# Another order for the parts of a software-pipelined stage: layer 1's cross-attention and experts

## The chip, the cores and the metric

The kernel runs on one core of one Trainium2 chip. The core has five engines with an instruction queue each: TensorE (PE, with the weight loads PEld beside it), VectorE (DVE), ScalarE (ACT), GpSimd (POOL) and SyncE (SP), which here only starts DMAs. An engine takes its instructions in the order of its queue; engines wait for each other by semaphores. The metric is the device time of one execution in microseconds.

## What is computed

A decoder of two layers on x of 16 x 256 tokens of 128 numbers, with a context of 16 x 64 tokens. Each layer adds to x an attention, a cross-attention with the context, and a mixture of experts, each on a layer norm of x. The change lies in the last two of layer 1:

```python
def _L1_xattn_ref(x, latents, w_q, w_kv, w_out, b_out):   # x: the context; latents: layernorm(x)
    q = latents @ w_q.T
    k, v = jnp.split(x @ w_kv.T, 2, axis=-1)              # 16 heads of 8, 64 keys
    ...
    attn = jax.nn.softmax(jnp.einsum('blhd,bshd->bhls', q, k) * SCALE, axis=-1)
    out = jnp.einsum('bhls,bshd->blhd', attn, v).reshape(B, L, DIM)
    return out @ w_out.T + b_out

def _L1_ffn_ref(x, gate_w, wg, wu, wd, sg, su, sd):       # 8 experts, the best two of each token
    top_w, top_i = jax.lax.top_k(jax.nn.softmax(xt @ gate_w, axis=-1), TOP_K)
    ...                                                   # cw: the two shares, else 0
    h = jax.nn.silu(einsum('th,ehi->eti', xt, wg)) * einsum('th,ehi->eti', xt, wu)
    moe = einsum('eth,te->th', einsum('eti,eih->eth', h, wd), cw)
    return moe + (jax.nn.silu(xt @ sg) * (xt @ su)) @ sd
```

## The kernel before, in words

All of x stays in SBUF, as eight chunks of 512 tokens (two sequences, four tiles of 128 tokens). Layer 0, layer 1's attention and layer 1's last stage follow each other; the last stage works on the eight chunks. In it every token is put through all experts, two experts to a product, and the routing's shares are multiplied in.

The stage is cut into *parts*, small functions of one engine each, which are called in the order of a list written out by hand, PLAN (L2076). An entry such as `E3:0` is a part and its distance in chunks: in iteration c the part E3 is called for chunk c, `h2:2` for chunk c-2, `S0:-1` for chunk c+1. The loop goes over iterations and, in each, over the list; entries whose chunk does not exist are left out. The calls' order is the order in each engine's queue (the block is scheduled by hand, and only where it meets the attention before it are instructions mixed). So the list sets, for each engine on its own, what stands behind what; between engines the framework puts the semaphores.

The parts that the text speaks of, by engine, with their lines:

- PE: S0 to S3 scores of a tile (L1816), T transposes of the probabilities, in two halves of a tile (L1876: T30 is tile 3, half 0), V products with the values (L1894), Y output projection (L1910), P transposes of the shares (L1863), xt and xq transposes and queries of a chunk (L1465, L1477), ft transposes and fl router products (L1932, L1941), fw transposes of the routing weights (L1976), h0 to h4 the gate and up products (L2004: h0 the shared expert, h1 to h4 two experts each), d0 to d3 the down products of a tile (L2022).
- DVE: G the greatest score (L1823), B the subtraction of it (L1827), R sums (L1849, L1850), O and X what comes out of V and Y (L1902, X adds to x: L1916), xs and fs layer norm statistics (L1447, L1448), fg the choice of two experts (L1948, then L160 to L178: reduces, and products and comparisons of 128 x 32 numbers, each on the result of the one before), fq the shares (L1959 to L1969), m gate times up (L2011), z the sum that is written out (L2031).
- ACT: E the exponential (L1835), C copies of T out of PSUM (L1885), U of P (L1870), xc, xQ, fc, fW copies (L1469, L1483, L1936, L1981; fW also starts, on SP, the two DMAs that spread the routing weights over partitions, L1983, L1988), fn normalisation (L1923), a0 to a4 Silu of the gate (L2008), fe the exponential of the routing (L1953). Exponential and Silu come from two tables, and a load (ACT_TABLE_LOAD) stands between them.
- POOL: A first additions of a tile's probabilities (L1841, L1842), Q the shares of the heads (L1855), K keys spread by heads (L1489), xr and fr roots for the layer norms (L1453 to L1460), xb adds the output's bias to x (L1472), k1 to k4 the multiplication of the experts' products by the routing weights (L2017).

PSUM: the scores hold four banks, one tile `sx` for two tiles' scores; h holds a bank for the gate and one for up (free again after a and m); everything else that PE writes (xt, xq, T, V, Y, P, ft, fl, fw, d) takes turns in two buffers, `misc`. Each of these parts therefore waits until what the part two places before it wrote has been copied out: by ACT for T, P, xt, xq, ft and fw, by DVE for V, Y, fl and d.

Of the kernel before, what the change touches and what calls it, by code (L numbers as in the profile page):

```python
# [62 lines left out]
def kernel(ctx: ExitStack, tc: tile.TileContext, a: dict, out: bass.AP):  # L63
# [1734 lines left out]
    with ExitStack() as ph:  # L1798
# [271 lines left out]
        for n in range(NPE + 1):  # L2070
# [3 lines left out]
            PARTS[f"k{n}"] = lambda c, n=n: weighted(c, n)  # L2074

        PLAN = (  # L2076
            "A0:0 a1:2 fs0:1 V1:1 z1:3 O1:1 xq:-1 xs0:-1 S3:0 K0:-2 R0:0 Y1:1 m1:2 xQ:-1 X1:1 "
            "T21:0 fs1:1 C21:0 A1:0 h2:2 T10:0 G3:0 Q0:0 a2:2 xb:-1 m2:2 T11:0 fr:1 C10:0 h3:2 "
            "T00:0 C11:0 T01:0 B3:0 k2:2 a3:2 C00:0 S0:-1 R1:0 m3:2 k1:2 xr:-1 xs1:-2 C01:0 "
            "T20:0 fn:1 G0:-1 C20:0 Q1:0 A2:0 h4:2 a4:2 k3:2 B0:-1 m4:2 P0:0 V0:0 U0:0 O0:0 "  # L2080
            "k4:2 ft:1 S1:-1 Y0:0 fc:1 fl:1 R2:0 h0:1 G1:-1 a0:1 X0:0 Q2:0 d3:2 fg:1 z3:2 E3:0 "
            "T30:0 fe:1 B1:-1 A3:0 C30:0 d0:2 E0:-1 xt:-2 m0:1 z0:2 S2:-1 fq:1 xc:-2 R3:0 Q3:0 "
            "T31:0 d2:2 C31:0 fw:1 G2:-1 z2:2 h1:1 E1:-1 P1:0 K1:-2 fW:1 U1:0 d1:2 B2:-1 E2:-1 "
        )
        room["m"] = ps_m
        plan = [part.split(":") for part in PLAN.split()]
# [66 lines left out]
```

## Time and profile before

| what | value |
|---|---|
| median of 9 runs | 1445.43 us (1443.76 to 1450.71) |
| the profiled execution's own time | 1447.09 us |
| its span in the profile | 1445.4 us |
| granted TensorE clock over the span | 0.98 |
| layer 1's last stage in the trace | from about 1190 us to the end |
| busy in 1275 to 1300 us | PE 23.82, DVE 20.44, ACT 16.65, POOL 17.28 of 25 us |

How it is read. The profile is one execution; times are in us from its start. Lines such as "L1876 PE MATMUL tx<-ident,px" are the line of the code, the engine, the operation, and what it writes and reads. An arrow in brackets behind a number of a timeline is the idle time of the engine before the instruction, and what ended it. The chain of waits follows the work that ended last back from the end of the program, at each step to what released it.

### The profile page before, as it was taken

What the parts mean: (1) busy time and instruction counts of PE and PEld (TensorE: products, weight loads), DVE (VectorE), ACT (ScalarE), POOL (GpSimd) and SP (SyncE); (2) the same over time, 40 slices, a digit from 0 to 9 for tenths busy, and PEclk for the clock granted to TensorE, in tenths of its full rate; (3) what the DMA queues carried; (4) which work ended last, traced back from release to release, by engine and by line L of the source; (5) the groups of instructions that cost most, each with busy time, mean ns of one, the idle gap of its engine ahead of it and who ended that gap; (6) DMA issues with size and microseconds to landing.
All of it is one profiled execution on the core that took longest, in us unless ns stands there. A gap on an engine that the chain in (4) does not pass through costs nothing.

```text
span 1445.4 us, 37905 instructions
## 1 busy us (share of the span) xinstructions
PE 1360.0 (94%) x13169; PEld 993.3 (69%) x13169; DVE 1114.1 (77%) x4508; ACT 950.7 (66%) x2569; POOL 727.6 (50%) x1160
## 2 busy tenths in 40 slices
PE   6999999999999999899999969999999987899997
PEld 4777776767676766589999956666666654566664
DVE  6676777777677767777878758999999968888863
ACT  5777675757576767344333319999999975666652
POOL 7454657474747564545433334443334216677643
PEclk9999999999999999899999988999999998999999
DMA  6772000000000000357677520000000000121122
GB/s 157 237 250 61 2 13 5 7 10 4 14 2 16 2 16 2 101 181 221 211 245 238 179 63 16 17 12 15 17 2 2 2 2 1 30 68 44 38 67 52
DMA packets 79757, 94.82 MB, mean 66 GB/s; under 512 B 19488, under 2 KB 62752, under 8 KB 79568
## 3 DMA queue, kind: packets, MB, share of 16 engines
q1 hardware_dynamic: 64736, 45.20, 11.8%
q10 hardware_dynamic: 10512, 38.28, 8.4%
q0 software_dynamic: 4320, 8.92, 1.8%
q8 instruction: 106, 1.74, 0.5%
q14 instruction: 83, 0.68, 0.2%
HBM read 63.72 MB, written 28.65 MB: 64 GB/s over the span
## 4 chain that ended last, share of the span: by engine, by line
PE 65%; ACT 17%; DVE 10%; DMA 2%; issue 2%; POOL 2%; SPq 0%; POOLq 0%; DVEq 0%; ACTq 0%
ACT p L1670 8%; PE pqk L406 8%; PE s L461 5%; PE o L533 5%; PE y L438 4%; PE g L1316 4%; PE u L1316 4%; PE y L1334 4%; PE pv L423 3%; PE t L1688 3%; PE t L513 2%; PE s L1648 2%; PE o L1712 2%; ACT pT L1699 2%; PE g L2004 2%
## 5 line engine op out<-in xcount | busy, mean ns | idle before, releaser
L486 ACT ACTIVATE p<-p,nm 128x128 f32<-128x128 f32 (+1 forms) x512 | 227.8, 447 | 138.6 <-DVE nm L474 136.4
L497 POOL TENSOR_SCALAR p<-p,rs 128x128 f32<-128x128 f32 (+1 forms) x512 | 210.5, 427 | 163.9 <-DVE rs L495 139.3
L1670 ACT ACTIVATE p<-p,nm 128x256 f32<-128x256 f32 x512 | 220.9, 507 | 9.6 <-DVE nm L1659 8.5
L1659 DVE CUSTOM_DVE_ANT_0 p<-s,strip 128x256 f32<-128x256 f32 x512 | 186.7, 419 | 19.6 <-PE s L1648 18.4
L474 DVE CUSTOM_DVE_ANT_0 p<-s,strip 128x128 f32<-128x128 f32 (+1 forms) x512 | 158.2, 347 | 2.2 <-PE s L461 2.2
L522 DVE COPY pT<-t 128x384 f32<-128x384 f32 x256 | 130.7, 552 | 27.8 <-PE t L513 26.9
L1344 POOL DMA_INDIRECT rows_out<-yr,to x71 | 68.5, 964 | 118.1 <-DVE yr L1343 111.0
L461 PE MATMUL s<-k,q 64*128 64x128 f32 (+1 forms) x1024 | 118.5, 350 | 0.0
L1688 PEld LDWEIGHTS t<-ident,p 64*128 64x128 f32 x2048 | 80.0, 140 | 54.2 <-issue 15.7
L533 PE MATMUL o<-pT,v 128*64 128x256 f32 (+1 forms) x1024 | 112.2, 340 | 0.5 <-ACT oT L543 0.5
L461 PEld LDWEIGHTS s<-k,q 64*128 64x128 f32 x1024 | 67.1, 186 | 62.5 <-issue 56.3
L1688 PE MATMUL t<-ident,p 64*128 64x64 f32 x2048 | 102.2, 232 | 7.8 <-ACT pT L1699 2.8
L432 DVE COPY v<-pv 128x512 f32<-128x512 f32 x64 | 44.1, 689 | 73.7 <-PE pv L423 73.6
L486 ACT ACTIVATION_READ_ACCUMULATOR p<-p,nm 128x1 f32 x512 | 96.8, 189 | 0.0
L1324 ACT ACTIVATE gs<-gs 128x512 f32<-128x512 f32 x71 | 44.7, 629 | 77.7 <-DVE gs L1323 64.2
L1648 PE MATMUL s<-k,q 32*128 32x256 f32 x1024 | 88.3, 418 | 4.5 <-POOL k L1568 4.5
L1530 POOL TENSOR_SCALAR ve_a<-mv_a 128x2 f32<-128x2 f32 x16 | 3.7, 229 | 164.3 <-DVE mv_a L1525 164.3
L1699 ACT COPY pT<-t 128x512 f32<-128x512 f32 x144 | 81.2, 588 | 5.5 <-PE t L1688 4.7
L513 PEld LDWEIGHTS t<-ident,p 64*128 64x128 f32 x1536 | 70.5, 139 | 19.1 <-DVE v L432 3.6
L533 PEld LDWEIGHTS o<-pT,v 128*64 128x64 f32 x1024 | 62.4, 136 | 28.2 <-ACT oT L543 0.9
L809 POOL DMA_INDIRECT rows_in<-xn,slot_in x64 | 63.7, 995 | 33.0 <-DVE nm L474 19.2
L1699 DVE COPY pT<-t 128x512 f32<-128x512 f32 x112 | 75.3, 684 | 5.9 <-PE t L1688 5.9
(341 smaller groups left out, 3403.5 us busy)
## 6 DMA issues: line engine op xcount, KB each, us to landing
gu<-in_L_ffn_gate_up_w ACTq DMA_DIRECT2D x71, 512.0 KB
rows_in<-zero SPq DMA_DIRECT2D x131, 130.0 KB
spread<-wrows SPq DMA_DIRECT2D x16, 512.0 KB
xr<-rows_in SPq DMA_DIRECT2D x71, 65.0 KB
y<-rows_out SPq DMA_DIRECT2D x16, 256.0 KB
x<-in_x SPq DMA_DIRECT2D x8, 256.0 KB
out_x<-yo SPq DMA_DIRECT2D x16, 128.0 KB
rows_out<-yr,to POOLq DMA_INDIRECT x71, 3.3
```

The costliest lines, as they stand in the source:

```text
L406: nc.tensor.matmul(ps[:, u, :], w[:, (pair + u) * P : (pair + u + 1) * P], xnT[b // 2][:, lo : lo + N], start=True, stop=True,)
L461: nc.tensor.matmul(ps_of[b, h][:, cols], q[rows, u2, iq], k[rows, u2, 0:nk], start=True, stop=True,)
L474: nc.vector.tensor_tensor_reduce(out=pr[:, cols], in0=ps[:, cols], in1=strip[:, h, P : 2 * P] if it == 0 else strip[:, h, :], scale=1.0, s ...
L486: nc.scalar.activation(pr[:, cols], pr[:, cols], AF.Exp, bias=nm[:, it : it + 1], scale=-1.0, accum_out=sm[:, it : it + 1],)
L497: nc.gpsimd.tensor_scalar(pr[:, cols], pr[:, cols], rs[:, it : it + 1], 1.0, ALU.mult, ALU.mult)
L522: nc.vector.tensor_copy(pT_of[u][:, :, :, r, :], tp_of[u][r])
L533: nc.tensor.matmul(po[rows, c0:N], v[:, jt, h % 8 * DH : (h % 8 + 1) * DH], pT[:, 0:N] if jt == 0 else pT[:, N:], start=(jt == 0), stop=(j ...
L1648: nc.tensor.matmul(ps_of[b, h][:, it, :], q[rows, it * P : (it + 1) * P], k[rows, s4, :], start=True, stop=True,)
L1659: nc.vector.tensor_tensor_reduce(out=pr[:, it, :], in0=ps[:, it, :], in1=strip1[:, h, (1 - it) * P : (1 - it) * P + N], scale=1.0, scalar= ...
L1670: nc.scalar.activation(pr[:, it, :], pr[:, it, :], AF.Exp, bias=nm[:, it : it + 1], scale=-1.0)
L1688: nc.tensor.transpose(halves[r][:, k, jt, it, :], pr[rows, it, jt * P : (jt + 1) * P], ident[rows, rows],)
L1699: copy(pT_of[u, i][:, :, :, :, r, :].rearrange("p k j i c -> p (k j i) c"), tp_of[u, i][r].rearrange("p k j i c -> p (k j i) c"),)
```

## The change

Only the list PLAN is another one (L2076). It has the same 105 parts. Four distances change: A0 from 0 to -1 (it stands at the end of the list and no longer at the head, the same chunk either way), xb from -1 to 0, K0 from -2 to -3, K1 from -2 to -1. All else is order:

```diff
         PLAN = (
-            "A0:0 a1:2 fs0:1 V1:1 z1:3 O1:1 xq:-1 xs0:-1 S3:0 K0:-2 R0:0 Y1:1 m1:2 xQ:-1 X1:1 "
-            "T21:0 fs1:1 C21:0 A1:0 h2:2 T10:0 G3:0 Q0:0 a2:2 xb:-1 m2:2 T11:0 fr:1 C10:0 h3:2 "
-            "T00:0 C11:0 T01:0 B3:0 k2:2 a3:2 C00:0 S0:-1 R1:0 m3:2 k1:2 xr:-1 xs1:-2 C01:0 "
-            "T20:0 fn:1 G0:-1 C20:0 Q1:0 A2:0 h4:2 a4:2 k3:2 B0:-1 m4:2 P0:0 V0:0 U0:0 O0:0 "
-            "k4:2 ft:1 S1:-1 Y0:0 fc:1 fl:1 R2:0 h0:1 G1:-1 a0:1 X0:0 Q2:0 d3:2 fg:1 z3:2 E3:0 "
-            "T30:0 fe:1 B1:-1 A3:0 C30:0 d0:2 E0:-1 xt:-2 m0:1 z0:2 S2:-1 fq:1 xc:-2 R3:0 Q3:0 "
-            "T31:0 d2:2 C31:0 fw:1 G2:-1 z2:2 h1:1 E1:-1 P1:0 K1:-2 fW:1 U1:0 d1:2 B2:-1 E2:-1 "
+            "a1:2 xq:-1 V1:1 fs0:1 R0:0 z1:3 O1:1 S3:0 xs0:-1 m1:2 Y1:1 xQ:-1 X1:1 T21:0"
+            " C21:0 h2:2 T10:0 G3:0 fs1:1 a2:2 K1:-1 Q0:0 A1:0 fr:1 m2:2 T11:0 C10:0"
+            " h3:2 T00:0 B3:0 C11:0 a3:2 C00:0 xs1:-2 R1:0 m3:2 S0:-1 S1:-1 T01:0 T20:0"
+            " fn:1 G0:-1 C01:0 C20:0 A2:0 Q1:0 h4:2 R2:0 B0:-1 P0:0 V0:0 a4:2 U0:0 O0:0"
+            " m4:2 G1:-1 xr:-1 xb:0 k3:2 k2:2 k1:2 k4:2 ft:1 Y0:0 fc:1 fl:1 h0:1 E3:0"
+            " a0:1 X0:0 d3:2 fg:1 z3:2 d0:2 T30:0 fe:1 A3:0 K0:-3 Q2:0 C30:0 m0:1 z0:2"
+            " B1:-1 d2:2 xt:-2 fq:1 E0:-1 xc:-2 z2:2 R3:0 Q3:0 A0:-1 S2:-1 fw:1 T31:0"
+            " G2:-1 h1:1 E1:-1 fW:1 C31:0 P1:0 U1:0 d1:2 B2:-1 E2:-1"
         )
```

By engine, the middle of an iteration reads so in the built program:

- PE before: V1 xq S3 Y1 T21 h2 T10 T11 h3 T00 T01 S0 T20 h4 P0 V0 ft S1 Y0 fl h0 d3 T30 d0 xt S2 T31 d2 fw h1 P1 d1. After: xq V1 S3 Y1 T21 h2 T10 T11 h3 T00 S0 S1 T01 T20 h4 P0 V0 ft Y0 fl h0 d3 d0 T30 d2 xt S2 fw T31 h1 P1 d1.
- ACT before: ... U0 fc a0 E3 fe C30 E0 xc C31 E1 fW U1 E2. After: ... U0 fc E3 a0 fe C30 E0 xc E1 fW C31 U1 E2.
- POOL before: A0 K0 A1 Q0 xb fr k2 k1 xr Q1 A2 k3 k4 Q2 A3 Q3 K1. After: K1 Q0 A1 fr A2 Q1 xr xb k3 k2 k1 k4 A3 K0 Q2 Q3 A0.
- DVE before: fs0 z1 O1 xs0 R0 m1 X1 fs1 G3 m2 B3 R1 m3 xs1 G0 B0 m4 O0 R2 G1 X0 fg z3 B1 m0 z0 fq R3 G2 z2 B2. After: fs0 R0 z1 O1 xs0 m1 X1 G3 fs1 m2 B3 xs1 R1 m3 G0 R2 B0 O0 m4 G1 X0 fg z3 m0 z0 B1 fq z2 R3 G2 B2.

## The prediction

> **What bounds the kernel now.** I read the page first, for the share of each engine, and then the windows over stretches of the last stage (layer 1's cross-attention and experts, from about 1190 us to the end). The windows' columns are the length, then busy us and count of PE, PEld, DVE, ACT and POOL, the clock and the DMA.
>
> ```profile
> PE 1360.0 (94%) x13169; PEld 993.3 (69%) x13169; DVE 1114.1 (77%) x4508; ACT 950.7 (66%) x2569; POOL 727.6 (50%) x1160
> ```
> ```profile
> 1275.00:1300.00 25.00, 23.82 (x179) 15.74 (x178) 20.44 (x59) 16.65 (x28) 17.28 (x21) 1.00 0.15 39
> 1300.00:1325.00 25.00, 23.82 (x173) 15.85 (x172) 20.51 (x55) 16.71 (x28) 18.50 (x24) 1.00 0.13 31
> ```
>
> PE is busy 23.82 of 25 us at full clock: the stage is PE's. The chain of waits in order of time shows where the missing 1.18 us is.
>
> ```profile
> 1339.66 0.97 PE g L2004 x2
> ...
> 1341.27 1.28 ACT L1835
> ...
> 1342.57 1.16 ACT px L1835
> ...
> 1343.77 0.65 PE tx L1876 x4
> ...
> 1367.62 0.97 PE g L2004 x2
> ```
>
> An iteration is 1367.62 - 1339.66 = 27.96 us. ACT waits for the first expert product, does its Silu (a0), loads a table (the nameless 1.28 us), and only then comes the exponential E3, for which PE's transposes T30 wait. The waits from 1225 to 1350 us agree (us in total, times, longest).
>
> ```profile
> POOL half L1841 <- ACT px L1835: 19.9, 5, 4.9
> ...
> ACT gs L2008 <- PE g L2004: 12.9, 13, 2.5
> ...
> PE tx L1876 <- ACT px L1835: 7.0, 5, 2.3
> ```
>
> PE stalls 2.29 us in the stage's first full iteration (at 1232) and 1.18 us in six more. The first row matters as much: POOL waits for E3 too, up to 4.9 us. What DVE does meanwhile is the routing fg (L1948, L160 to L178), thirteen small dependent instructions, 2.73 us (1339.76 to 1342.49). The timelines of DVE and of POOL show why that idle POOL is worth something. First the end of the kernel, where POOL is not idle during fg; then the first iteration, where fq, the second half of the routing, meets POOL.
>
> ```profile
> 1415.28 1.32 DVE L162 TENSOR_TENSOR eq_f<-lgs_f,m_f 128x32 f32<-128x32 f32 x1
> 1416.63 0.19 DVE L163 TENSOR_TENSOR eq_f<-eq_f,rev 128x32 f32<-128x32 f32 x1
> ```
> ```profile
> 1411.61 4.95 POOL L2017 TENSOR_TENSOR hb<-hb,spread 128x512 f32<-128x512 f32 x4 [1.21 <-DVE hb L2011]
> ```
> ```profile
> 1232.61 0.98 DVE L1959 TENSOR_SCALAR w<-dm_f 128x4 f32<-128x4 f32 x1
> ...
> 1233.83 0.56 DVE L1961 TENSOR_TENSOR dm_f<-dm_f,w 128x4 f32<-128x4 f32 x1
> ```
> ```profile
> 1232.27 1.29 POOL L1841 TENSOR_TENSOR half<-px 128x512 f32<-128x512 f32 x1 [4.92 <-ACT px L1835]
> 1233.64 0.73 POOL L1842 TENSOR_TENSOR half<-half 128x256 f32<-128x256 f32 x1
> ```
>
> L162 takes 0.19 us elsewhere; here 1.32, and it ends at 1416.60, just behind POOL's last product (1416.56). L1959 (0.16 elsewhere) ends at 1233.59, behind POOL's 1233.56, and L1961 (0.16) at 1234.39, behind 1234.37. So a small DVE instruction of this kind (two SBUF inputs, or L1959's form) stands still until the POOL instruction under way ends. The reduces between them (L160, L167) and those that read PSUM run on at their usual lengths.
>
> **The change, part by part.** Same parts, so nothing is removed; the list moves them.
>
> *E3 before a0.* E3's input is long there, so it fills the 2.45 us in which ACT waited for the product: fc ends, table 1.28, E3 1.15, all before PE has done the first product pair and d3, d0 (0.81 + 1.80 + 1.12 + 1.12 = 4.85 us from the start of fl). The stall of 1.18 goes. The built program has 34 table loads for 22: two more in each of six iterations, 2 x 1.28 us of ACT. They lie before a0 and before fe, where ACT was waiting; ACT then stands about where it stood (C30 0.9 us after T30's start, xt's slot free 0.1 us before PE wants it). I cost them at nothing; without that cover they cost up to 2.56 us an iteration.
>
> *Small new waits on PE.* S1 leaves the place between ft and fl, and only Y0 (0.55) covers fc there. The last full iteration of before has no S1, and shows the price: from the start of V0 (1390.10) to fl (1392.43) 2.33 us for 1.00 + 0.58 + 0.55 of work, so +0.20. xq goes ahead of V1, so Y1 now waits for the PSUM slot of xq: U1, E2 1.15, table 1.29, a1 0.49, xQ 0.59 after P1 is 4.06 us, against d1 1.21, xq 1.05, V1 1.00 and S3 0.65: +0.15. Keys, S0 with S1, R0 and R2: their inputs are ready 0.3 us or more ahead, nothing. SP's copies keep their order; the weights land 9 us after fW (1238.28 to 1247.30), and the first product comes 15 after it (fW 5.8 ahead of X1, the product 9.6 behind X1, see below): 6 to spare, nothing.
>
> *POOL's order.* Count from X1 (L1916, at 1355.24 in before). In before fs1 ends 1.35 later and POOL's row of fr, products, xr, Q1, A2, products, Q2 ends at 1367.92, X1 + 12.68; fg's first L162 is issued at X1 + 12.92, and then POOL idles for E3. After: G3 stands ahead of fs1 (+1.10), so fs1 ends at 2.45. POOL: fr 2.06, A2 2.06, Q1 0.36, xr 1.32, xb 1.25 (moved here), and now all four products in a row, 4 x 1.25; the third ends at 13.34, the fourth at 14.59. As E3 is early, A3 follows at once (2.06), then K0 0.60 and Q2 0.37. PE from the end of Y1 to the end of fl is 12.45 + 0.20; X1 starts 0.6 behind Y1, so fl ends at X1 + 12.05. DVE must finish G1 and X0 first (V0's end, O0, m4, G1, X0 give 12.55); L162 is issued at about 12.95.
>
> So fg, until now beside an idle POOL, meets 4.7 us of POOL work in a row. Eight of its instructions can stand still. If each gets in behind the POOL instruction under way: L162 13.4, L163 14.7 (fourth product), L169 16.0 and L175 16.9 (A3), L162 17.5 (K0), L163 17.9 (Q2), the rest free: fg ends at 18.5 and not 15.3. z3 (0.29) follows, and frees the PSUM slot that T30 needs: T30 at 18.9, while PE is ready for it at 12.05 + 1.80 + 1.12 + 1.12 = 16.1. A stall of 2.8 where 1.18 went. d2 then waits for m0 and z0 behind z3 (19.8, PE at 19.4): +0.4.
>
> *Sum of an iteration:* -1.18 + 0.20 + 0.15 + 2.8 + 0.4 = +2.4 us. Six such (the last has no S, but the same row of POOL work): +14.2.
>
> *Ends.* First iteration: the stall of 2.29 goes, but fg meets A3, K0 and Q2, B1 stands behind fg, and S2 behind B1 comes at 1234.3 as before (1234.22): 0, between -2.3 and +1. The fill gains S1's place beside older work, -0.25. The last two iterations hold no A3 and no S, and hang on the copy of the weights to 1431.3 as before: 0. In all +14 on the profiled execution, whose own time is 1447.09 us (span 1445.4); that is 1.66 above the median, so 1445.4 + 14 = 1459.5.
>
> *Bounds of the disputed step.* That no row shows DVE waiting in a long row of POOL instructions leaves it open from both sides. Below: if fg is not held, it ends at 15.3, z3 at 15.6, T30 doesn't wait; -0.8 an iteration, -5 in all, about 1440. Above: if DVE gets in only when POOL runs dry (17.6), fg ends at 19.95, T30 at 20.3: stall 4.2, +3.8 an iteration, +23, 1468. I take the turn-by-turn value by its nearest row: L1959, issued within L1841, ended (1233.59) before L1842 began (1233.64).
>
> The Trainium skill (SBUF — State Buffer, "Who interferes with whom") says that a VectorE instruction with two SBUF inputs and a GpSimd instruction that reads SBUF exclude each other for the whole instruction, and that the order of issue decides who waits. The rows above show the first half; no run here shows the order of issue in a long row of GpSimd work. By that rule a waiting VectorE instruction is ahead of the next GpSimd one, which is the 1459.5; were the row of GpSimd work to keep the port, it would be the 1468.
>
> **The rivals.**
> - *E3's stall simply goes; fg finds POOL idle or isn't held.* 1440, faster. For it: the stall is real, and three of the stage's five meetings of DVE and POOL (1233.83, 1256.34, 1393.97) cost under 0.4 us. Against: A3 alone follows E3 by 0.05 us and covers 2.06 us of fg. It decides if POOL's row ends before X1 + 13. Chance 0.15.
> - *POOL keeps the port till it runs dry.* 1468. For it: L162 at 1415.28, issued as the last product was, lost the whole of it. Chance 0.12.
> - *ACT becomes the bound by its two loads*, with no hold-up on DVE: 6 x (2.56 - 1.18) = +8, 1453.5. Against: ACT is busy 16.6 of 25. Chance 0.05.
> - *A partial hold-up*: only A3's first instruction costs, stall 1.0 to 1.6, -0.2 to +0.8 an iteration: 1444 to 1450. Chance 0.08, half of it within 0.2%.
>
> **How the numbers follow.** 0.2% (2.9 us) is about what a measurement of this kernel tells from no change. Forecast 0.60, at 1459.5. Slower: 0.60 + 0.12 + 0.05 + 0.04 = 0.81; same 0.04; faster 0.15. Between 1440 and 1468 lie all the cases, so the range is that; the likeliest case alone spans 1453 to 1465.
>
> **What would show it.** Right: T30 no longer waits for ACT but for DVE (yo L2031), 2 to 4 us in six iterations; L162, L163, L169 and L175 stretch to 0.5 to 1.4 us and end with POOL's instructions; POOL's wait for E3 is gone; an iteration of some 30.4 us. Wrong: L162 and L163 at 0.19 throughout and iterations of 27.2; or T30 waiting for the table loads; or the stall moved to Y1 or fl by more than 0.2.

## The result, and the profile after

The kernel after takes 1457.37 us (median of 10 runs, 1453.66 to 1461.62), the kernel before, run beside it, 1445.54 (median of 30). The ratio is 1.0077, 95% interval 1.0064 to 1.0090: slower by 0.8%, where 1459.5 was forecast. The profiled execution is the shortest on record: 1453.06 us, span 1451.3.

First the page's line of the engines.

```profile
PE 1360.7 (94%) x13169; PEld 994.1 (68%) x13169; DVE 1125.7 (78%) x4508; ACT 965.7 (67%) x2581; POOL 727.0 (50%) x1160
```

PE is as busy as before, ACT has 15 us more (twelve table loads). The waits from 1225 to 1400 us tell more.

```profile
POOL rs L1855 <- DVE smx L1850: 31.5, 10, 4.9
...
PE tx L1876 <- ACT dm_f L1953: 9.4, 5, 2.0
...
ACT gs L2008 <- PE g L2004: 2.9, 12, 0.3
...
ACT dm_f L1953 <- DVE dm_f L178: 6.5, 6, 1.2
```

In the steady iterations POOL no longer waits for E3, nor ACT for the first product. But PE still stalls ahead of T30, 9.4 us in five turns, up to 2.0 each. The row names fe (dm_f, ACT) as the releaser; when an instruction waits for several events, the row names the one that came last. Here are PE, DVE and POOL of one iteration.

```profile
1287.49 1.06 PE L2022 MATMUL yf<-wd,hb 128*128 128x128 f32 x8
1290.46 0.63 PE L1876 MATMUL tx<-ident,px 128*128 128x128 f32 x4 [1.91 <-ACT dm_f L1953]
1291.16 0.49 PE L2022 MATMUL yf<-sd,hb 128*128 128x128 f32 x2
1291.48 1.42 PE L2022 MATMUL yf<-wd,hb 128*128 128x128 f32 x8
```
```profile
1285.15 0.54 DVE L162 TENSOR_TENSOR eq_f<-lgs_f,m_f 128x32 f32<-128x32 f32 x1
1285.73 1.19 DVE L163 TENSOR_TENSOR eq_f<-eq_f,rev 128x32 f32<-128x32 f32 x1
1286.95 0.19 DVE L167 TENSOR_REDUCE mi_f<-eq_f 128x4 f32<-128x32 f32 x1
1287.18 0.98 DVE L169 TENSOR_TENSOR eq_f<-eq_f,mi_f 128x32 f32<-128x32 f32 x1
1288.19 0.19 DVE L175 SCALAR_TENSOR_TENSOR rest_f<-eq_f,lgs_f 128x32 f32<-128x32 f32 x1
...
1288.64 0.38 DVE L162 TENSOR_TENSOR eq_f<-rest_f,m_f 128x32 f32<-128x32 f32 x1
1289.06 0.54 DVE L163 TENSOR_TENSOR eq_f<-eq_f,rev 128x32 f32<-128x32 f32 x1
...
1290.03 0.28 DVE L2031 TENSOR_TENSOR yo<-x,yf 128x128 f32<-128x128 f32 x1
```
```profile
1281.92 4.95 POOL L2017 TENSOR_TENSOR hb<-hb,spread 128x512 f32<-128x512 f32 x4
1286.83 1.29 POOL L1841 TENSOR_TENSOR half<-px 128x512 f32<-128x512 f32 x1
1288.19 0.78 POOL L1842 TENSOR_TENSOR half<-half 128x256 f32<-128x256 f32 x1
1288.94 0.61 POOL L1489 TENSOR_TENSOR kb<-kTx,rmask 128x256 f32<-128x256 f32 x1
```

Lay the second beside the third. L163 ends at 1286.92, behind the fourth product (1286.87); L169 at 1288.16, behind A3's first addition (1288.12); the second L162 at 1289.02, behind its second (1288.97); the second L163 at 1289.60, behind K0 (1289.55). L175 started in the same moment as A3's second addition (1288.19) and kept its 0.19. The reduce L167, in the middle of A3, keeps its length. So fg takes 5.4 us instead of 2.72; z3 (yo) ends at 1290.31, and T30 starts at 1290.46. fe was itself waiting for fg, and T30 does not read what fe writes.

The iterations, from the start of one fl to the next, in us:

| | to 1st fl | 1 | 2 | 3 | 4 | 5 | 6 | 7 | rest |
|---|---|---|---|---|---|---|---|---|---|
| before | 1227.18 | 27.65 | 27.96 | 27.95 | 27.96 | 27.95 | 25.78 | 21.30 | 31.61 |
| after | 1226.41 | 28.17 | 28.86 | **30.45** | 28.90 | 28.69 | 27.08 | 22.07 | 30.72 |

The steady iterations (2 to 5) cost 0.7 to 0.9 us more, and one of them 2.5. That one begins at 1283.44, the one shown: behind its stall the products of d2 took 1.42 us where those ahead of it took 1.06. The windows of that place (length, then PE, PEld, DVE, ACT, POOL, the granted clock, the DMA) give the reason.

```profile
1288.60:1292.00 3.40, 1.47 (x11) 1.26 (x12) 3.26 (x10) 1.54 (x4) 1.31 (x3) 1.00 0.00 0
1292.00:1295.40 3.40, 3.40 (x20) 2.23 (x20) 2.26 (x11) 2.35 (x3) 1.33 (x2) 0.50 0.13 39
1295.40:1298.80 3.40, 3.40 (x21) 2.34 (x19) 3.26 (x8) 1.75 (x5) 1.62 (x3) 1.00 0.03 5
```

The granted clock is 0.50 for 3.4 us, which is 1.7 us of work lost. That stood in no step of the prediction. (The kernel before has one such stretch too, in its first iteration, from 1232.2, behind E3's stall of 2.29.)

### The profile page after: what moved, and what is told of

Read it like the earlier page. It is cut to its first block, busy times and chain, and to the rows that moved or that the text cites. A ratio compares the mean times of both kernels' runs of the same rounds, so it can differ in the third digit from the quotient of the medians.

```text
span 1451.3 us, 37913 instructions
## 1 busy us (share of the span) xinstructions
PE 1360.7 (94%) x13169; PEld 994.1 (68%) x13169; DVE 1125.7 (78%) x4508; ACT 965.7 (67%) x2581; POOL 727.0 (50%) x1160
## 4 chain that ended last, share of the span: by engine, by line
PE 64%; ACT 16%; DVE 13%; issue 2%; DMA 2%; POOL 1%; SPq 0%; POOLq 0%; DVEq 0%; ACTq 0%
ACT p L1670 8%; PE pqk L406 8%; PE s L461 5%; PE o L533 5%; PE g L1316 4%; PE y L438 4%; PE y L1334 4%; PE u L1316 4%; PE pv L423 3%; PE t L1688 3%; PE t L513 2%; PE s L1648 2%; ACT pT L1699 2%; PE o L1712 2%; PE g L2004 2%
## 5 line engine op out<-in xcount | busy, mean ns | idle before, releaser
L1659 DVE CUSTOM_DVE_ANT_0 p<-s,strip 128x256 f32<-128x256 f32 x512 | 186.6, 419 | 19.9 <-PE s L1648 18.3
L522 DVE COPY pT<-t 128x384 f32<-128x384 f32 x256 | 130.7, 552 | 27.3 <-PE t L513 26.5
L533 PEld LDWEIGHTS o<-pT,v 128*64 128x64 f32 x1024 | 62.4, 136 | 28.9 <-ACT oT L543 1.6
```

Source lines behind the costliest of these rows:

```text
L522: nc.vector.tensor_copy(pT_of[u][:, :, :, r, :], tp_of[u][r])
L533: nc.tensor.matmul(po[rows, c0:N], v[:, jt, h % 8 * DH : (h % 8 + 1) * DH], pT[:, 0:N] if jt == 0 else pT[:, N:], start=(jt == 0), stop=(j ...
L1659: nc.vector.tensor_tensor_reduce(out=pr[:, it, :], in0=ps[:, it, :], in1=strip1[:, h, (1 - it) * P : (1 - it) * P + N], scale=1.0, scalar= ...
```

## The experiments

Theory: POOL's instructions hold up fg's on DVE, so z3 and T30 come late. Rivals: the twelve added table loads; the small waits at Y1, Y0 and fl. The second theory, formed on the profile after: the longer stalls of PE bring stretches at half clock. The experiments ran on two chips on which the kernel before takes 1470.60 and 1471.62 us (the kernel after, profiled here and there, comes to its last stage some 26 us later on the second of them; its first and last iterations agree within 0.1 us, 28.17 and 28.16, 22.07 and 22.09). Each ratio is to the kernel before in the same runs.

| kernel | loads | fg, us | stall ahead of T30, us | iteration, us | ratio |
|---|---|---|---|---|---|
| before | 22 | 2.72 | 1.18 | 27.96 | 1 |
| after | 34 | 5.2 to 5.5 | 1.7 to 2.0 | 28.7 to 28.9 (30.45 once) | 1.0077 |
| far_operand | 34 | 2.43 | 0 | 26.66 | 0.9931 (0.9909 to 0.9954) |
| e3_late | 22 | 3.7, 4.1 or 5.2 | 0.2, 0.6 or 1.7 | 27.5 to 28.7 | 1.0005 (0.9992 to 1.0019) |
| e3_early_alone | 34 | 3.9 or 4.3 | 0 (d0: 0.9 or 1.3) | 27.7 or 28.1 | 0.9972 (0.9957 to 0.9988) |
| t30_late | 22 | 2.86 | 0 (P0: 0.7 to 0.9) | 27.9 | 1.0016 (1.0002 to 1.0030) |
| after_again | 34 | 5.2 to 5.7 | 1.7 to 2.2 | 30.3 to 30.8 | 1.0097 (1.0078 to 1.0116) |
| warm | 34 | 5.4 | 0.2 | 29.06 | 1.0049 (1.0036 to 1.0062) |
| k_early | 34 | 4.2 | 0.73 | 27.74 | 1.0008 (0.9998 to 1.0018) |
| t30_late_k | 22 | 2.72 | 0 | 26.91 | 0.9970 (0.9956 to 0.9984) |

Behind the loads, which are those of the whole kernel, the columns up to the iteration are over the steady iterations (2 to 5).

**far_operand.** In fg, with E3 early and POOL's row as in after (the line of the helper that fg calls, against the line written in its place):

```diff
+            far = sx[:, 0, 0, 0:1, 0:32].rearrange("p o (t e) -> p (o t) e", t=TPC)
...
-            nc.vector.tensor_tensor(
-                eq, eq, rev.unsqueeze(1).to_broadcast([P, nt, E]), ALU.mult
-            )
+                nc.vector.tensor_tensor(eq, eq, far, ALU.mult)
```

and so for all eight instructions with two tensors in SBUF.

> The kernel after, with one thing changed: every instruction of fg that had two inputs in SBUF now reads its second one from the scores' PSUM bank (same shapes, same number of instructions; the choice of experts is then not the router's, so that part of the computation is left out). The list, POOL's work and the table loads stay. Theory (POOL's instructions hold up fg's instructions with two SBUF inputs, fg ends late, z3 and T30 follow): L162, L163, L169, L175 of after (0.4 to 1.2 us each) become 0.2 to 0.25 here, fg takes 2.7 to 3.2 us instead of 5.4, PE's stall ahead of T30 falls from 1.9-2.1 us to 0 to 0.3, an undisturbed iteration from 28.8 to 26.9-27.3 us; 1442 to 1447 us in all. Rival (the added table loads or the small waits make after slow): fg's length is not what T30 waits for, the stall stays at 1.9 and the time at 1457.

DVE and POOL of one iteration, then the window of one stretch:

```profile
1305.15 0.19 DVE L1961 TENSOR_TENSOR eq_f<-eq_f,sx 128x32 f32<-128x32 f32 x1
...
1305.60 0.19 DVE L1964 TENSOR_TENSOR eq_f<-eq_f,sx 128x32 f32<-128x32 f32 x1
...
1306.80 0.19 DVE L1964 TENSOR_TENSOR eq_f<-eq_f,sx 128x32 f32<-128x32 f32 x1
```
```profile
1301.85 4.95 POOL L2041 TENSOR_TENSOR hb<-hb,spread 128x512 f32<-128x512 f32 x4
1306.76 1.28 POOL L1841 TENSOR_TENSOR half<-px 128x512 f32<-128x512 f32 x1
```
```profile
1300.00:1325.00 25.00, 24.97 (x184) 16.37 (x183) 21.05 (x63) 19.41 (x29) 18.22 (x23) 1.00 0.24 55
```

The same POOL row lies over fg (products to 1306.80, then A3), and no instruction of fg takes more than 0.19. With that the stall is gone, and PE is busy 24.97 of 25 us with all 34 table loads in place. In the first iteration PE still idles 1.57 us, at S2. This decides between the theory and both rivals. The gain was larger than expected (26.66 us instead of 26.9 to 27.3): no other wait shows up behind z3's. Some 0.3 us of fg's 2.43 is another effect: the comparisons no longer wait for m_f, as they don't read it.

**e3_late.** In PLAN of after:

```diff
-h0:1 E3:0 a0:1 X0:0
+h0:1 a0:1 E3:0 X0:0
```

> The kernel after with one part put back: a0 ahead of E3 (22 table loads instead of 34; A3, K0 and Q2 again wait for a late E3). Theory (fg held up by POOL): of after's 2.7 us of hold-up in fg the 1.3 us from A3, K0 and Q2 go, the 1.35 us from the products k stay; z3 then ends 0.85 us behind PE's last work ahead of T30, E3 about as late; the stall is 0.6 to 1.0 us, an iteration 27.6 to 27.9 us, 1449 to 1452 us. Rival (table loads): all that after lost goes with the twelve loads and the old stall of 1.18 comes back: 1445 to 1446, with fg still as long as in after. Rival (small waits at Y1, Y0 and fl): 1456 to 1458.

A ratio of 1.0005, less than the theory's 1449 to 1452 (1.0025 to 1.0045 of before), and close to what the rival with the table loads gave; the stall is 0.6 in some iterations as expected, but 1.7 in others and 0.2 in one. Where it is 1.7, A3 comes just ahead of fg's last instruction:

```profile
1369.57 1.25 POOL L1841 TENSOR_TENSOR half<-px 128x512 f32<-128x512 f32 x1 [1.73 <-ACT px L1835]
```
```profile
1369.61 1.24 DVE L178 TENSOR_TENSOR dm_f<-m_f,m_f 128x4 f32<-128x4 f32 x1
```

Issued 0.04 us behind it, sixteen bytes a partition wait 1.24 us. The products' part of the hold-up is in all iterations (L163 took 1.19 at 1338.89). Undoing E3's move alone thus brings the time back, but the rival's mechanism is not there: T30 waits for fg and z3 and not for E3 (at 1342.30, where E3 had ended at 1341.71), fg stays at 3.7 to 5.2 us, and a steady iteration still takes 28.2 us on average for before's 27.96. The first takes 0.4 less (27.25), and, unlike in after, no stretch at half clock falls into the steady ones. Why the ratio comes out quite so low is not settled beyond that.

**e3_early_alone.** In PLAN of before:

```diff
-h0:1 G1:-1 a0:1 X0:0 Q2:0 d3:2 fg:1 z3:2 E3:0 T30:0
+h0:1 G1:-1 E3:0 a0:1 X0:0 Q2:0 d3:2 fg:1 z3:2 T30:0
```

> The kernel before with one part of the change alone: E3 ahead of a0 (34 table loads, POOL's order as in before). Theory (port): POOL's products and Q2 end before fg's first comparison as in before, but A3 now starts during fg (about 2.4 us behind fl's start) and covers 2.06 us of it: fg becomes 1.0 to 1.9 us longer, T30, here called right behind d3, waits for z3 until 5.1 to 6.0 us after fl's start instead of 5.07 for E3: 1445 to 1451 us, so no gain although E3's stall is gone. Rival (fg is not held): z3 ends 4.1 us behind fl's start, the stall shrinks to 0.2, 1439 to 1440 us. Rival (ACT bound by the loads): 1453, with T30 or C30 waiting for ACT.

```profile
1364.04 1.20 DVE L169 TENSOR_TENSOR eq_f<-eq_f,mi_f 128x32 f32<-128x32 f32 x1
```
```profile
1363.91 1.28 POOL L1841 TENSOR_TENSOR half<-px 128x512 f32<-128x512 f32 x1 [0.82 <-ACT px L1835]
```
```profile
1337.48 0.60 PE L1876 MATMUL tx<-ident,px 128*128 128x128 f32 x4
1339.37 0.49 PE L2022 MATMUL yf<-sd,hb 128*128 128x128 f32 x2 [1.29 <-DVE yo L2031]
```

E3's stall is gone, but A3 holds L169, and now d0, not T30, waits for z3: an iteration takes 27.7 or 28.1 us for 27.96, so there is no gain from what looked like a stall of 1.18. The ratio of 0.9972 is below the expected 1445 to 1451 (1.000 to 1.004). The first iteration, which I had left out of the sum, gained 2.1 us (25.52 for 27.65): PE stalls 1.78 there, at S2, instead of 2.29, and the stretch at half clock that follows in before (1.7 us of work) does not come; one falls ahead of this iteration, at 1248.2.

**t30_late.** In PLAN of before (d2 goes with it, to behind T30; on DVE m0 and z0 go ahead of B1, and z2 ahead of S2):

```diff
-z3:2 E3:0 T30:0 fe:1 B1:-1 A3:0 C30:0 d0:2
+z3:2 d0:2 E3:0 T30:0 fe:1 A3:0 C30:0
```

> The kernel before, POOL's order and E3 behind a0 as they were; only d0 (on PE) is called ahead of T30 instead of behind it, with m0 and z0 ahead of B1 and z2 ahead of S2 on DVE, so that PE has 1.12 us of work where it waits for E3. Theory (in before only E3's lateness costs the 1.18 us, and POOL must be left idle during fg): the stall ahead of T30 shrinks from 1.18 to 0.1-0.2 us, fg stays at 2.7 us, an iteration 26.9 to 27.1 us: 1438.5 to 1441 us, below both kernels. Rival (fg's or another wait takes its place: d2, T31 or S2 wait for m0, z0, C30): 1444 to 1447.

A miss: T30 no longer waits in the steady iterations, and nothing is won. The wait that took its place is none of those named. POOL's and PE's timelines, one iteration:

```profile
1330.04 2.49 POOL L2017 TENSOR_TENSOR hb<-hb,spread 128x512 f32<-128x512 f32 x2 [1.68 <-DMA spread<-wrows]
...
1333.91 0.41 POOL L1855 TENSOR_TENSOR rs<-ones,smx 128x128 f32<-128x128 f32 x1
```
```profile
1334.38 0.33 PE L1863 MATMUL rt<-ident,rs 128*128 128x128 f32 x1 [0.80 <-POOL rs L1855]
```

The first products k2 and k1 wait for the copy of the routing weights, Q1 stands behind them on POOL, and PE's P0 waits for Q1. In before, the same products start with next to no wait; the first row below shows them, the two blocks behind it SP's copies, first in before (fl at 1310.75), then in t30_late (fl at 1309.48):

```profile
1330.74 2.51 POOL L2017 TENSOR_TENSOR hb<-hb,spread 128x512 f32<-128x512 f32 x2
```
```profile
1321.44 0.30 SPq L1983 DMA_DIRECT2D wrows<-cTf  x1
1322.97 1.24 SPq L1988 DMA_DIRECT2D spread<-wrows  x2
```
```profile
1320.14 0.30 SPq L1983 DMA_DIRECT2D wrows<-cTf  x1
1321.91 0.37 SPq L2038 DMA_DIRECT2D out_x<-yo  x1
1322.38 1.24 SPq L1988 DMA_DIRECT2D spread<-wrows  x2
```

So two things meet. In before the copy has nothing to spare: in the steady iterations the products start 19.9 to 20.0 us behind fl, with a wait of 0.12 at most. In t30_late POOL comes to them a good 1.0 us earlier (18.9 behind fl), and the copy comes later: the store of z0 and z1 (L2038) now stands between its two steps on SP, which start the second one 12.90 behind fl instead of 12.2. The second part is this edit's own doing and no property of before; which share of P0's 0.7 to 0.9 each has, no run separates.

**t30_late_k.** To test whether the copy is what t30_late waits for, on top of t30_late:

```diff
-B3:0 k2:2 a3:2 C00:0 S0:-1 R1:0 m3:2 k1:2 xr:-1 ... Q1:0 A2:0 h4:2
+B3:0 a3:2 C00:0 S0:-1 R1:0 m3:2 xr:-1 ... Q1:0 A2:0 k2:2 k1:2 h4:2
```

> The kernel t30_late (before, with d0 ahead of T30), with the products k2 and k1 moved on POOL behind xr, Q1 and A2. In t30_late k2 waited 1.68 us for the copy of the routing weights, Q1 stood behind it, and PE's P0 waited 0.7 to 0.9 us for Q1: that took the place of the stall ahead of T30. Theory (the copy of the weights is the second bound of before, hidden behind the first): the wait goes, P0 no longer stalls, an iteration takes 26.8 to 27.2 us, with fg still 2.7 to 3.0 us long; ratio to before 0.994 to 0.997. Rival (POOL's whole row, not the copy, is the bound): iterations stay at 27.7 to 27.9, ratio 0.999 to 1.002.

```profile
1300.00:1325.00 25.00, 24.94 (x186) 16.59 (x185) 21.65 (x64) 16.65 (x26) 17.94 (x24) 1.00 0.23 55
```
```profile
1325.81 4.96 POOL L2017 TENSOR_TENSOR hb<-hb,spread 128x512 f32<-128x512 f32 x4
1330.73 0.40 POOL L1855 TENSOR_TENSOR rs<-ones,smx 128x128 f32<-128x128 f32 x1
1335.02 1.29 POOL L1841 TENSOR_TENSOR half<-px 128x512 f32<-128x512 f32 x1 [3.88 <-ACT px L1835]
```

POOL's work is the same, and so are the lateness of E3 and the store on SP; only the place of two products differs. No wait for the copy in the steady iterations, PE busy 24.94 of 25, 26.91 us an iteration: the copy was t30_late's bound, not POOL's row. What the expectation calls the second bound of before is shown as that of t30_late; of before, the traces show only that its copy has no slack. With POOL idle during fg (1331.1 to 1335.0) this version is faster than both kernels (0.9970).

**k_early.** In PLAN of after:

```diff
-X1:1 T21:0 C21:0 h2:2 T10:0 G3:0 fs1:1 a2:2 K1:-1 Q0:0 A1:0 fr:1
+X1:1 fs1:1 T21:0 C21:0 h2:2 T10:0 G3:0 a2:2 K1:-1 Q0:0 A1:0 xb:0 fr:1
...
-xr:-1 xb:0 k3:2 ... A3:0 K0:-3 Q2:0 ... A0:-1 S2:-1
+xr:-1 k3:2 ... A3:0 Q2:0 ... A0:-1 K0:-3 S2:-1
```

> The kernel after, with POOL's row finished ahead of fg: xb ahead of fr, where POOL idles, fs1 ahead of T21 again (fr starts about 1.1 us earlier), and K0 behind A0; E3 stays early. Theory (fg is held up by what POOL does beside it): the four products end before fg's first comparison, and only A3 and Q2 (2.4 us) are left to meet it; fg takes 3.7 to 4.4 us instead of 5.4, the stall ahead of T30 is 0.4 to 0.8 us, an iteration 27.2 to 27.6 us, ratio to before 0.995 to 0.998. Rival (table loads or small waits): 28.3 to 28.8 us, ratio 1.004 to 1.008.

fg 4.2 us and the stall 0.73, as expected; A3 alone still takes 1.0 from L175 (1.18 us at 1339.75) and 0.36 from the second L162. The iteration is 0.14 us above the range, because PE's work between the stalls takes 27.0 us in this order and I had counted 26.8; and the first iteration (28.82 us) has a new stall at S2, 2.85 us with 6.8 us at half clock behind it. So the ratio, 1.0008, misses the expected 0.995 to 0.998. Half confirmed: the length of fg and the stall are, the time is not; and the rival's iterations of 28.3 to 28.8 are out.

**after_again and warm.** Both are about the clock. The first is the kernel after once more; the second, with a part for two products thrown away:

```diff
+        def again(c):
+            nc.tensor.matmul(held["u"], su1, held["xTf", c], start=True, stop=True)
...
-z3:2 d0:2 T30:0
+z3:2 d0:2 w0:1 w1:1 T30:0
```

> The kernel after, unchanged, once more: a second profile and a second set of times. In the first profile one of the steady iterations cost 30.45 us instead of 28.8, because the granted clock was 0.5 for 3.41 us right behind the stall ahead of T30. Clock theory (the 1.9 us stalls of after bring such stretches, in some iterations of each execution, other ones each time): undisturbed iterations of 28.7 to 28.9 us, one to three stretches at half clock among them, a mean clock 0.001 to 0.003 below that of the kernel before, ratio 1.006 to 1.010. Rival (that stretch was chance, and has nothing to do with the change): no such stretch, the same mean clock as before, ratio 1.003 to 1.005, which is what six or seven iterations of +0.9 us make.

> The kernel after, with two products of the shared expert's up weights (0.86 us each, results thrown away) put on PE behind d0, into the time in which PE waits for T30. Nothing is left out. PE's stall shrinks from 1.9 to 0.1-0.3 us though z3 and T30 come no earlier, so an undisturbed iteration stays at 28.7 to 29.0 us. Clock theory (PE's idleness brings the stretches at half clock): none in the steady iterations, mean clock as in the kernel before or above, ratio 1.003 to 1.006, 2 to 7 us below the kernel after of the same runs. Rival (the stretches have another cause): times equal to those of the kernel after within 1 us, or slower.

First after_again, windows around its stalls; then warm, and what stands in its stall.

```profile
1285.80:1289.20 3.40, 1.43 (x11) 1.03 (x10) 3.19 (x12) 1.55 (x3) 1.31 (x3) 1.00 0.00 0
1289.20:1292.60 3.40, 3.40 (x18) 3.07 (x22) 2.62 (x10) 1.70 (x3) 0.14 (x1) 0.50 0.00 0
1316.50:1319.90 3.40, 1.10 (x9) 0.70 (x7) 3.19 (x12) 1.21 (x3) 1.66 (x3) 1.00 0.00 0
1319.90:1323.30 3.40, 3.40 (x18) 3.07 (x22) 2.73 (x10) 1.62 (x3) 0.00 (x0) 0.50 0.00 0
```
```profile
1275.00:1300.00 25.00, 24.55 (x165) 15.67 (x164) 21.31 (x56) 18.02 (x26) 15.48 (x18) 1.00 0.22 54
1300.00:1325.00 25.00, 24.55 (x174) 15.46 (x173) 21.49 (x53) 19.08 (x30) 19.18 (x25) 1.00 0.09 23
```
```profile
1313.42 1.88 PE L2007 MATMUL u<-xTf,su 128*128 128x512 f32 x4
1315.50 0.63 PE L1876 MATMUL tx<-ident,px 128*128 128x128 f32 x4 [0.20 <-ACT dm_f L1953]
```

After_again has five such stretches (from 1261.9 in the first iteration, behind a stall at S2, and from 1289.2, 1319.9, 1350.6 and 1381.3, each behind a stall at T30): the four steady iterations take 30.3 to 30.8 us, where they last 28.8 undisturbed. That is more than the one to three expected, and the mean clock over the runs is 0.9707 against 0.9762 before, a fall of 0.0055 where 0.001 to 0.003 was expected. In warm, fg, z3 and T30 are as late as in after, an iteration takes 29.06 us (0.2 of it a new wait of d2 for z0), and no stretch at half clock follows; its mean clock is 0.9792, and its median 5.2 us below that of after_again, though it does more work. So idle PE brings these stretches, and they are about half of what after_again loses: 1.0049 without, 1.0097 with them (warm also takes 2.7 us longer behind the last fl, so this is no exact split).

## Why the prediction was right, and where not

The direction and the time were right (1457.4 for 1459.5, inside the 1453 to 1465 of the likeliest case). Its steps one by one:

- *The stall of 1.18 goes with E3 before a0; the loads cost nothing.* Right: E3 ends at 1285.85, 2.7 us ahead of PE's need (1288.55), and far_operand has the 34 loads and no stall in its steady iterations.
- *POOL's row lies over fg.* Right to 0.3 us, counted from X1 (1272.49 here): the fourth product ends at 14.38 (forecast 14.59), PE is ready for T30 at 16.06 (16.1), fg's first comparison is issued at 12.66 (12.95).
- *DVE gets in turn by turn.* Right, and the rival in which POOL keeps DVE out until it runs dry is wrong: L163, L169 and the second L162 and L163 each ended within 0.05 us of one POOL instruction's end, the first of them 3 us before POOL ran dry (1289.91). The Trainium skill (SBUF — State Buffer, "Who interferes with whom") calls the ports that the two engines share an exclusive lock and has the order of issue decide who waits; the rows above agree (L163, issued within the fourth product, took 1.19 us, to that product's end), and so does far_operand, whose instructions with one input outside SBUF kept 0.19 us.
- *A stall of 2.8 at T30.* The term that was mis-sized: it measured 1.7 to 2.0. I had six instructions held, the last to X1 + 17.9 by Q2; in the iteration shown L175 was not held, the second L163 met K0 instead of Q2, and fg ended at X1 + 17.6 and not 18.5.
- *+0.20 and +0.15 at Y1 and fl, +0.4 at d2.* Too large: no such gap of 0.1 us shows in the steady iterations; an iteration less its stall is 27.0 us instead of 26.8, so they come to 0.2 in all. An undisturbed iteration is therefore not +2.4 but 1.9 - 1.18 + 0.2, some +0.9.
- *The sum.* The +2.4 came about all the same in disturbed iterations (30.3 to 30.8), by a term that I did not have: the stretch at half clock, +1.7. The six iterations that were to cost 14.2 us more (2 to 7) cost 7.2 in the profile of after, with one such stretch, and 12.1 in that of after_again, with four (both against the one profile of before). That the forecast median is so close is thus partly luck. Two terms were too big, one was missing, and they cancel.
- *First iteration 0; last ones 0.* The first costs 0.5 more; the end behind the last fl gained 0.9 and the beginning 0.8. Small. Iterations 6 and 7, which the sum has at +2.4 each, cost 1.1 to 1.3 and 0.8. In the first, S2 comes 7.1 us after fl as forecast: a stall of 3.38 there for E3's 2.29.
- *6 us to spare for the weights' copy.* It held in after, where the products stand last on POOL. In before's order there is nothing to spare, and t30_late, whose copy also starts 0.7 us later, waits for it as soon as E3's stall is gone. So the new place of the products, which I priced only by what it does to fg, also keeps them clear of the copy: far_operand has no such wait in its steady iterations.
- *The rival in which fg is not held, 1440.* Its condition was wrong, its price nearly right and rather too high: far_operand, which meets the condition, has 0.9931, that is 1435.5 on the scale of 1445.5.

## To carry to other kernels

An idle engine may be what keeps another fast: before a wait is taken away that keeps GpSimd quiet, list which VectorE instructions with two SBUF inputs will then run beside it, however small they are, and price each at the rest of the GpSimd instruction under way. When a stall is removed and nothing is won, look for the next wait in line, here a copy through DRAM that had no slack, and look whether the edit itself has moved something in another engine's queue. And price a TensorE stall not by its length alone: here stalls of 1.7 to 2.2 us cost another 1.7 us wherever a stretch at half clock followed.

## What the runs showed of the hardware that was not expected

The stretches at half clock come in steps of 3.41 us on one grid throughout an execution (1234.0 and 1292.0 us in after are 17 steps apart). Counted on that grid, in the steady iterations of all ten profiles, every step in which PE was idle for 1.79 us or more (1.79, 1.93, 1.97, 1.99, 2.30) is followed by a step at half clock, and none in which it was idle for 1.72 or less (1.72, 1.68, 1.68, 1.63, and all those of 1.18 in before). In the first iteration it is less clean: steps with 1.82, 2.12, 2.23, 2.29 and 2.96 us were followed by one, but one with 1.78 was not (e3_early_alone). Ahead of the first iteration the count fails: there a step with 1.49 was followed by one (e3_early_alone, at 1244.8), and in five profiles one with only 0.5 to 0.8 (after_again at 1214.1: 0.52). So idle time alone is not the rule; what else counts, no run here shows. For the steady iterations the limit lies near half of the step, and a stall counts only as far as it falls into one step. That fits the profile of after, whose stalls of 1.7 to 2.0 lie at changing places of the grid and have one such stretch, and after_again, whose steady iterations have four, 30.72 us apart: that is just nine steps, so that the next stall can fall on the same place again. It need not: in after the stall behind the disturbed one put only 1.68 us into one step, and no stretch followed. This reading of the places is argued from the times, not tested.

The Trainium skill (TensorE: Matmul & The Clock Gate, "HAM oscillation — how this bites in real kernels") gives as its rule that there be no idle gaps of TensorE above about 3.4 us. Here gaps of 1.9 us were enough, with 1.47 us of work in the same step. By that rule the steady iterations of after would have had no such stretch, and its second set of times would be near the 1.0049 of warm; the measured 1.0097 decides.
